# A macaron block with experts on one core: first layernorm's statistics partly on ACT, the last additions shared between engines, a priority for each pair and block

## The chip, the cores and the metric

The kernel runs on one core of a Trainium2 chip. The metric is device time in microseconds, from the launch of the one program to its end; the time given is the median of three runs. The engines are PE (matrix products and transposes), DVE (vector), ACT (activations), POOL (vector work and indirect DMAs) and SP (which only issues DMAs here).

## The reference

All arithmetic is in float32, on x with 2 x 2048 tokens of 256 numbers each:

```python
x = x + 0.5 * ffn(layernorm(x))
x = x + attention(layernorm(x))
x = x + 0.5 * ffn(layernorm(x))

# ffn: 8 experts of width 176, the best 2 for each token
probs = softmax(h @ router_w.T); vals, idx = top_k(probs, 2)
vals = vals / vals.sum(-1)
for each expert e:
    gate, up = split(h @ gate_up_proj[e].T)
    out += weight_of_e * ((silu(gate) * up) @ down_proj[e].T)

# attention: a causal convolution over 3 tokens gives q, k, v of width 64;
# 8 heads of 64, causal softmax within blocks of 128 tokens,
# then two projections (64, 256)
```

## The kernel before, in words

**Stages.** The 4096 tokens are 8 groups of 512, each of 4 tiles of 128 tokens. The first feed-forward (half 1) runs in two chunks, groups 0 to 2 and 3 to 7; then each group's attention; then the second feed-forward (half 2) in chunks of groups 0 to 4 and 5 to 7. In names of tiles, `hs_f1_0_4` is half 1, chunk 0, from slot 4.

**Layernorm.** `layernorm()` makes a group's means and variances half a group (two tiles) at a time: two `bn_stats` (L505) and two `bn_aggr` (L507) on DVE. The power -0.5 is taken on POOL (L520), after an addition on DVE (L515); where ACT does the normalising (L548), POOL also makes a shift (L527, L528), and DVE normalises at L543. The result goes to DRAM (`hd`), and through transposes (L564, copied out as hT) into the router's logits (L638, L652).

**Routing.** `route()` finds the two best experts, counts, and places each token in slots of 128 rows that belong to one expert. This is a long list of small DVE instructions (L697 to L912), then for each pair of token tiles a one-hot step on DVE (L977, L981, L985) and four products (psl, L992), whose sums are the indices (L1010; second chunk L1019, L1023). The table of the slots' experts (L928 to L952) is read by PE and SP into registers, for each pair anew.

**Experts.** `expert()` handles two slots (a pair): POOL gathers their rows by index (L1113, `hs`), PE transposes them (L1124, `ptr`, copied out as hsT), multiplies with gate and up (L1165, `pgu`), ACT does the tanh (L1179), DVE the rest of swiglu (L1185 to L1188), PE transposes (L1195/1196, `pm`, copied out as hmT) and multiplies with the down projection (L1218/1224, `po`), copied out as `ys`. The three copies go through a helper, on ACT at L295 and on DVE at L299. In half 1 the pairs are stored (`yd`) and gathered by `combine()` (POOL L1329, DVE addition L1339). In half 2 POOL scatters them to DRAM (L1240, a put); `gather_all()` then loads, for two tiles of tokens at a time, 512 KB (SP L1283, into one of four buffers "s"), adds four times on DVE (L1304, weight times row plus x) and stores the result (SP L1314).

**Attention.** For each group: convolution (pqk L1515, pv L1537), pvm (L1556), pu (L1609), then four blocks of 128 tokens: scores (ps L1633), mask (L1642, DVE), row maxima (L1651 to L1653, DVE), exponential (L1667, ACT), reciprocal (L1674, DVE), the product with it (L1678, POOL), transposes (pst L1688), context (pcx L1705), projection (pp L1725), and the addition to x (L1735, DVE). POOL adds the projection's bias to x at L1496.

**What sets the order.** Nothing is issued in the order of the source. Each call of `step()` records a piece of work with its cost on one or more engines (the first named is its main engine; another one is taken only where the main one is busy for over 0.3 us longer). `Plan.emit()` then lays all steps out as a list on every engine, in modelled time: of the steps that could start first, the one of highest priority goes. Priority is the longest modelled path to the end plus a bias, which the table `RANK` sets for each stage. Steps also wait for free buffers of their pool. The list of each engine is then fixed, so on the chip an instruction that waits holds up all that stand behind it on its engine. While the plan finds PE idle in the first 60 us, it fills the gap with `warm` products.

The rule for the choice of engine, and the bias of the pairs:

```python
main = next(iter(s.costs))
if e != main and free[main] < t + 0.3:
    continue
...
plan.bias = RANK["expert1"][c] - 0.1 * RANK["slope1"][c] * i
expert(k, i, min(2, k.NSL - i))
```

Of the kernel before, what the change touches and what calls it, by code (L numbers as in the profile page):

```python
# [10 lines left out]
AF = mybir.ActivationFunctionType  # L11
# [10 lines left out]
NS = TB // P  # L22
# [35 lines left out]


RANK = {  # L60
    "logits1": (2852, 2216, 3314, 3481, 1963, 1827, 1743, 3136),
    "route1": (2091, 3734),
    "expert1": (1442, 1598),
    "fold": -360,
    "combine1": (18, 283, -268, 352, -138, -584, -694, -436),
    "attention": (31, 66, 458, -108, 359, -125, -210, -806),
    "logits2": (342, -30, -17, 461, -107, 728, -336, -232),
    "route2": (-70, 1682),
    "expert2": (-795, -757),
    "combine2": (-359, -989),  # L70
    "slope1": (168, 1),
    "slope2": (10, 184),
}


# [171 lines left out]
def kernel(  # L247
# [38 lines left out]
    def work(tag, shape, name, dt=F32):  # L286
        return buf(pools[tag], tag, shape, name, dt)
# [208 lines left out]
    def layernorm(g, nm, store, hT, off, wide=None):  # L496
        stats = work("stats", [P, NS, 6], f"stats_{nm}")
        mv = work("mv", [P, NS, 2], f"mv_{nm}")
        rstd = work("rstd", [P, NS], f"rstd_{nm}")
        for i in range(NH):  # L500
            ts = range(2 * i, 2 * i + 2)

            def stat(e, ts=ts):
                for t in ts:
                    nc.vector.bn_stats(stats.t[:, t, :], X[g].t[:, t, :])  # L505
                for t in ts:
                    nc.vector.bn_aggr(mv.t[:, t, :], stats.t[:, t, :])  # L507

            step(
                {"DVE": 0.89}, stat, reads=[(X[g], t) for t in ts],  # L510
                writes=[(stats, i), (mv, i)],
            )
        step(
            {"DVE": 0.1},
            lambda e: nc.vector.tensor_scalar(rstd.t, mv.t[:, :, 1], EPS, None, ALU.add),  # L515
            reads=[mv], writes=[rstd],
        )
        step(
            {"POOL": 1.1},
            lambda e: nc.gpsimd.tensor_tensor(rstd.t, rstd.t, mhalf.t, ALU.pow),  # L520
            reads=[mhalf], writes=[rstd],
        )

        shift = work("shift", [P, NS], f"shift_{nm}")

        def shifts(e):
            nc.gpsimd.tensor_tensor(shift.t, mv.t[:, :, 0], rstd.t, ALU.mult)  # L527
            nc.gpsimd.tensor_scalar(shift.t, shift.t, -1.0, None, ALU.mult)  # L528

        step({"POOL": 0.25}, shifts, reads=[mv, rstd], writes=[shift])  # L530
        for i in range(NH):
            if wide is None:
                h = work("h", [P, 2, D], f"h_{nm}_{i}")
                h_ = lambda h=h: h.t
            else:
                h, h_ = wide, lambda i=i: wide.t[:, 2 * i : 2 * i + 2, :]
            hp = (h, i)

            def norm(e, i=i, h_=h_):
                for j in range(2):  # L540
                    t = 2 * i + j
                    if e == "DVE":
                        nc.vector.tensor_scalar(  # L543
                            h_()[:, j, :], X[g].t[:, t, :], mv.t[:, t, 0:1],
                            rstd.t[:, t : t + 1], ALU.subtract, ALU.mult,
                        )
                    else:
                        nc.scalar.activation(  # L548
                            h_()[:, j, :], X[g].t[:, t, :], AF.Identity,
                            bias=shift.t[:, t : t + 1], scale=rstd.t[:, t : t + 1],  # L550
                        )

            step(
                {"ACT": 0.98, "DVE": 0.65}, norm,
                reads=[rstd, mv, shift] + [(X[g], 2 * i + j) for j in range(2)], writes=[hp],
            )
            if store is not None:
                store(i, hp, h_)
            pt = bank([P, KD, 2, P], f"pt_{nm}_{i}")

            def turn(e, h_=h_, pt=pt):
                for c in range(KD):
                    for j in range(2):
                        nc.tensor.transpose(  # L564
                            pt.t[:, c, j, :], h_()[:, j, c * P : (c + 1) * P], ident.t
                        )

            step({"PE": 0.52}, turn, reads=[hp, ident], writes=[pt], room=[hT])
            o0 = off + 2 * i * P
            step(  # L570
                {"ACT": 0.49, "DVE": 0.6},
                lambda e, pt=pt, o0=o0: copy(
                    e, hT.t[:, :, o0 : o0 + 2 * P].rearrange("p c (t q) -> p c t q", q=P),
                    pt.t,
                ),
                reads=[pt], writes=[(hT, i)],
            )
        return rstd
# [511 lines left out]
    def expert(k, i0, n):  # L1090
        nm = f"{k.nm}_{i0}"

        beside = k.half == 2 and k.first

        def copied(act, dve):
            return {"ACT": act, "DVE": dve} if beside else {"DVE": dve, "ACT": act}
# [174 lines left out]
    def gather_all(g):  # L1271

        k = chunk_of(g, 2)
        want = [(k, i) for i in range(k.NSL)]
        if k.first:
            want += [(k.next, i) for i in range(NLEFT)]
        for t in range(0, NS, 2):
            n = (g - k.g0) * NS + t
            yg = work("s", [P, 2, 2, D], f"y2_{g}_{t}")

            def get(e, t=t, yg=yg):
                r0 = 2 * (g * TB + t * P)
                ins = nc.sync.dma_start(  # L1283
                    yg.t, Y2.t[r0 : r0 + 4 * P, :].rearrange("(t p j) d -> p t j d", p=P, j=2)
                )
                apart(ins, [m for w, m in Y2.puts.items() if w not in want])
                for w in want:
                    tc.add_manual_dep(
                        ins.ins, Y2.puts[w],
                        mybir.DependencyInfo(  # L1290
                            mybir.DependencyClass.Sync, mybir.DependencyReason.DATA
                        ),
                        reason="its rows",
                    )
                Y2.gets.append(ins.ins.name)

            step(
                {"SP": 0.5}, get, reads=[(Y2, w) for w in want], writes=[yg], lat=LAND, kb=512
            )
            for i in range(2):  # L1300
                for j in range(2):
                    step(
                        {"DVE": 0.43},
                        lambda e, i=i, j=j, n=n, t=t, yg=yg: nc.vector.scalar_tensor_tensor(  # L1304
                            X[g].t[:, t + i, :], yg.t[:, i, j, :],
                            k.wt.t[:, j, n + i : n + i + 1], X[g].t[:, t + i, :],
                            ALU.mult, ALU.add,
                        ),
                        reads=[yg, k.wt], writes=[(X[g], t + i)],
                    )  # L1310
            r0 = g * TB + t * P
            step(
                {"SP": 0.35},
                lambda e, r0=r0, t=t: nc.sync.dma_start(  # L1314
                    out[r0 : r0 + 2 * P, :].rearrange("(t p) d -> p t d", p=P),
                    X[g].t[:, t : t + 2, :],
                ),
                reads=[(X[g], t), (X[g], t + 1)], lat=LAND, kb=256,
            )
# [154 lines left out]
    def attention(g):  # L1474
# [145 lines left out]
                )  # L1620

        oT = work("oT", [P, NS // 2, P], f"oT_{nm}")
        for b in range(NS):
            bs = slice(b * P, (b + 1) * P)

            s = work("s", [P, HEADS, P], f"s_{nm}_{b}")
# [113 lines left out]
    for c in range(2):  # L1740
        k = chunks[1, c]
        for g in range(k.g0, k.g1):
            plan.bias = RANK["logits1"][g]
            logits(g, 1)
            if c == 0 and g == k.g1 - 1:
                loads_then(k.rows)
        plan.bias = RANK["route1"][c]
        route(k)
        for i in range(0, k.NSL, 2):
            plan.bias = RANK["expert1"][c] - 0.1 * RANK["slope1"][c] * i  # L1750
            expert(k, i, min(2, k.NSL - i))
            if c == 0 and i == 0:
                step({"PE": 0.1}, ones_once, reads=[(k.y, 0), ones16], writes=[warm])
                plan.bias = RANK["expert1"][c] + 500.0
                hand_on(k)
                loads_last(k)
# [9 lines left out]
    for c in range(2):  # L1766
        k = chunks[2, c]
        plan.bias = RANK["route2"][c]
        route(k)
        for i in range(0, k.NSL, 2):  # L1770
            plan.bias = RANK["expert2"][c] - 0.1 * RANK["slope2"][c] * i
            expert(k, i, min(2, k.NSL - i))
            if c == 0 and i == 0:
                hand_on(k)
# [66 lines left out]
```

## Time and profile before

| what | before |
| --- | --- |
| median of three runs | 714.97 us (713.4 to 716.16) |
| the profiled execution | 717.35 us, of which its span is 715.6 |
| PE busy | 650.9 us (91%), 4837 instructions |
| DVE busy | 512.4 us (72%), 1408 instructions |
| ACT busy | 317.6 us (44%), 1008 instructions |
| POOL busy | 398.6 us (56%), 458 instructions |
| chain that ended last | PE 54%, DVE 33%, issue 4%, POOL 4%, DMA 4%, ACT 1% |
| mean granted clock of PE | 0.946 |

The span runs from the first to the last instruction of the profiled execution. Busy shares are averages over stages that have different limits, so they don't say what bounds the kernel. The chain is followed back from the last instruction through whatever released each one. In a row of a group of instructions, the numbers before the bar are the total and the mean of one, and behind it stands the idle time of the engine ahead of them with what ended it.

### The profile page before, as it was taken

To read this page: it belongs to the slowest core of one execution; us is meant where nothing else is said; L and a number is where in the kernel's file an instruction comes from. 1 tells how busy PE (TensorE), PEld (TensorE's weight loads), DVE (VectorE), ACT (ScalarE), POOL (GpSimd) and SP (SyncE) were. 2 spreads that over 40 slices of the span, in tenths; PEclk is the share of its full clock that TensorE was granted. 3 is DMA by queue.
4 is the path that set the end of the run, shared out by engine and by line. 5 is a ranking of instruction groups with operands and counts; after the bars stand their busy time and mean duration, and the time that the engine had idled before them with its cause. 6 is when DMAs were issued, how large, how long until landed. Compare 5 with 4: busy or idle time off the path is not lost.

```text
span 715.6 us, 14981 instructions
## 1 busy us (share of the span) xinstructions
PE 650.9 (91%) x4837; PEld 492.9 (69%) x4837; DVE 512.4 (72%) x1408; ACT 317.6 (44%) x1008; POOL 398.6 (56%) x458
## 2 busy tenths in 40 slices
PE   6888989999999999799989997979999799999960
PEld 4647868888888754657566564657888687888840
DVE  5884984455448959998999789999845933447735
ACT  4224322222222437495997857448944233223220
POOL 4037207643337877787744622158867477777650
PEclk9699989999999999899999998979999899999995
DMA  9916616564456343023100110027224234439937
GB/s 295 305 63 188 225 49 181 181 181 142 131 139 177 123 119 88 24 59 105 38 32 30 29 47 15 17 80 231 86 87 140 65 118 131 126 110 322 323 109 264
DMA packets 64891, 92.59 MB, mean 129 GB/s; under 512 B 10128, under 2 KB 50352, under 8 KB 64720
## 3 DMA queue, kind: packets, MB, share of 16 engines
q1 hardware_dynamic: 51520, 55.31, 24.1%
q0 software_dynamic: 13296, 36.32, 17.3%
q8 instruction: 41, 0.67, 0.4%
q14 instruction: 34, 0.28, 0.1%
HBM read 56.47 MB, written 37.22 MB: 131 GB/s over the span
## 4 chain that ended last, share of the span: by engine, by line
PE 54%; DVE 33%; issue 4%; POOL 4%; DMA 4%; ACT 1%; SPq 0%; POOLq 0%; DVEq 0%; ACTq 0%
PE pgu_f L1165 20%; PE po_f L1218 8%; PE po_f L1224 5%; DVE nmx_a L1651 4%; DVE s_a L1642 4%; PE ptr_f L1124 3%; DVE x L1339 2%; PE pm_f L1195 2%; DVE oh_f L977 2%; PE pst_a L1688 2%; PE pcx_a L1705 2%; DVE stats_f L505 2%; PE pt_f L564 2%; POOL yg_f L1329 1%; DVE ot_f L985 1%
## 5 line engine op out<-in xcount | busy, mean ns | idle before, releaser
L1113 POOL DMA_INDIRECT hs_f<-hd_f,idx_f x142 | 137.1, 965 | 129.0 <-PE ptr_f L1124 40.6
L1165 PE MATMUL pgu_f<-wx,hsT_f 128*128 x1136 | 184.0, 318 | 1.8 <-DVE hsT_f L299 0.8
L1165 PEld LDWEIGHTS pgu_f<-wx,hsT_f 128*128 128x128 f32 x1136 | 172.7, 193 | 7.5 <-issue 2.6
L1667 ACT ACTIVATE s_a<-s_a,nmx_a 128x128 f32<-128x128 f32 x256 | 98.9, 392 | 11.8 <-DVE nmx_a L1653 11.2
L1678 POOL TENSOR_TENSOR s_a<-s_a,sm_a 128x512 f32<-128x512 f32 x64 | 67.0, 1069 | 61.4 <-DVE sm_a L1674 59.7
L1240 POOL DMA_INDIRECT y<-ys_f,dst_f x71 | 71.0, 1000 | 33.5 <-ACT ys_f L295 13.9
L295 ACT COPY ys_f<-po_f 128x256 f32<-128x256 f32 x123 | 40.8, 375 | 109.8 <-PE po_f L1224 92.4
L1179 ACT ACTIVATE hm_f<-pgu_f 128x352 f32<-128x352 f32 (+1 forms) x72 | 33.0, 460 | 108.8 <-PE pgu_f L1165 106.5
L1218 PE MATMUL po_f<-wx,hmT_f 128*128 x284 | 76.6, 392 | 0.7 <-DVE hmT_f L299 0.7
L1185 DVE SCALAR_TENSOR_TENSOR hm_f<-hm_f,pgu_f 128x352 f32<-128x352 f32 (+1 forms) x72 | 36.7, 510 | 56.2 <-ACT hm_f L1179 55.9
L1329 POOL DMA_INDIRECT yg_f<-yd_f,posi_f x64 | 61.7, 964 | 24.9 <-issue 15.3
L1218 PEld LDWEIGHTS po_f<-wx,hmT_f 128*128 128x128 f32 x284 | 49.5, 192 | 10.6 <-DVE hm_f L1188 3.3
L299 DVE COPY hmT_f<-pm_f 128x384 f32<-128x384 f32 x40 | 22.2, 556 | 44.1 <-PE pm_f L1196 43.9
L1224 PE MATMUL po_f<-wd_f,hmT_f 48*128 48x256 f32 x284 | 51.1, 432 | 0.0
L1339 DVE SCALAR_TENSOR_TENSOR x<-yg_f,wt_f,x 128x256 f32<-128x256 f32 x64 | 41.6, 674 | 11.0 <-DMA yg_f<-yd_f,posi_f 11.0
L1667 ACT ACTIVATION_READ_ACCUMULATOR s_a<-s_a,nmx_a 128x1 f32 x256 | 49.0, 192 | 0.0
L1515 PE MATMUL pqk_a<-haT_a,cw 128*128 128x512 f32 x96 | 46.3, 630 | 0.5 <-ACT haT_a L295 0.5
L1124 PE MATMUL ptr_f<-ident,hs_f 128*128 128x128 f32 x284 | 42.2, 276 | 2.4 <-DMA hs_f<-hd_f,idx_f 2.4
L1688 PE MATMUL pst_a<-ident,s_a 128*128 128x128 f32 x256 | 37.1, 287 | 4.5 <-DVE vm_a L299 2.9
L1642 DVE TENSOR_TENSOR s_a<-ps_a,later 128x512 f32<-128x512 f32 x64 | 40.5, 678 | 0.0
L1688 PEld LDWEIGHTS pst_a<-ident,s_a 128*128 128x128 f32 x256 | 29.2, 146 | 16.3 <-issue 9.5
L1651 DVE TENSOR_REDUCE nmx_a<-s_a 128x8 f32<-128x1024 f32 x32 | 38.7, 1210 | 0.2
(235 smaller groups left out, 1228.0 us busy)
## 6 DMA issues: line engine op xcount, KB each, us to landing
yd_f<-ys_f SPq DMA_DIRECT2D x42, 256.0 KB, 3.6
hd_f<-h_f SPq DMA_DIRECT2D x32, 256.0 KB, 3.2
y<-y SPq DMA_DIRECT2D x16, 512.0 KB, 5.3
wd_f<-in_w_down SPq DMA_DIRECT2D x142, 48.0 KB, 2.7
x<-in_x SPq DMA_DIRECT2D x16, 256.0 KB, 7.0
out<-x SPq DMA_DIRECT2D x16, 256.0 KB, 3.2
hd_f<-hd_f SPq DMA_DIRECT2D x1, 2560.0 KB
hs_f<-hd_f,idx_f POOLq DMA_INDIRECT x142
```

The source lines that it names most:

```text
L1113: lambda e, i=i, hs_=hs_: nc.gpsimd.indirect_dma_start(out=hs_(), out_offset=None, in_=k.h.t[:, :], in_offset=bass.IndirectOffsetOnAxis(ap ...
L1124: nc.tensor.transpose(pt.t[:, d, j, :], hs_()[:, d * P : (d + 1) * P], ident.t)
L1165: nc.tensor.matmul(pgu[f].t[:, j, :], hsT.t[:, d, j, :], wx.t[:, bass.ds(at + d * GU + f * H, H)], start=(d == 0), stop=(d == KD - 1),)
L1218: nc.tensor.matmul(po[j].t, hmT.t[:, j, :], wx.t[:, bass.ds(at + KD * GU, D)], start=True, stop=False,)
L1224: nc.tensor.matmul(po[j].t, hmT.t[r, n, :], wd.t[r, :], start=False, stop=True)
L1240: ins = nc.gpsimd.indirect_dma_start(out=Y2.t[:, :], out_offset=bass.IndirectOffsetOnAxis(ap=k.dst.t[:, i : i + 1], axis=0), in_=ys.t[:, j ...
L1329: lambda e, j=j, n=n, yg=yg: nc.gpsimd.indirect_dma_start(out=yg.t, out_offset=None, in_=k.y.t[:, :], in_offset=bass.IndirectOffsetOnAxis( ...
L1642: lambda e, h=hd[i], s=s, p=ps[i]: nc.vector.tensor_tensor(s.t[:, h, :], p.t, later.t.to_broadcast([P, NPAIR, P]), ALU.add,),
L1651: nc.vector.tensor_reduce(nmx.t, s.t, AX.X, ALU.max)
L1667: nc.scalar.activation(s.t[:, n, :], s.t[:, n, :], AF.Exp, bias=nmx.t[:, n : n + 1], accum_out=sm.t[:, c : c + 1],)
L1678: lambda e, s=s, sm=sm, h=hd[i]: nc.gpsimd.tensor_tensor(s.t[:, h, :], s.t[:, h, :], sm.t.unsqueeze(2).to_broadcast([P, NPAIR, P]), ALU.mu ...
L1688: nc.tensor.transpose(pt.t[:, c, :], s.t[:, i * NPAIR + c, :], ident.t)
```

## The change

The table `RANK` gets other numbers for all stages, and five new lists: one bias for each pair of slots (`pairs10` to `pairs21`, for half and chunk) and one for each of the 32 attention blocks (`blocks`). For groups 3 to 7 the statistics step of the first layernorm may go to ACT where DVE is busy; there it is made of sums that two activations accumulate, with the tile that takes the normalised rows later as scratch. The plan puts five half groups there: both of group 4, both of group 5, and one of group 6. In half 1's first chunk the copies hsT, hmT and ys get ACT as main engine (so far only half 2's first chunk had that). In the last chunk's additions 4 of 12 tiles of tokens are scaled in place on ACT (two activations) and added on POOL (two additions) instead of two times on DVE.

```diff
 RANK = {
-    "logits1": (2852, 2216, 3314, 3481, 1963, 1827, 1743, 3136),
+    "logits1": (3004, 3634, 3185, 2969, 1036, 1648, 1568, 3176),
...
+    "pairs10": (-38, 306, 165, -360, -358, -360, -818, 76, -597),
...
+    "blocks": (4, 4, 5, 4, 4, 4, 4, 4, 4, 4, 4, 4, 7, 4, -141, 4, 8, 494, -157, -7, 0, 0, 0, 0, 0, 0, 0, 0, 0, 114, -26, -1),
...
+        shared = wide is not None and g >= first
...
             def stat(e, ts=ts):
+                if e == "ACT":
...
+                    a = nc.scalar.activation
+                    st, m = stats.t, slice(ts[0], ts[-1] + 1)
+                    for t in ts:
+                        a(wide.t[:, t, :], X[g].t[:, t, :], AF.Identity, accum_out=st[:, t, 0:1])
+                    a(mv.t[:, m, 0], st[:, m, 0], AF.Copy, scale=1.0 / D)
+                    a(st[:, m, 1], st[:, m, 0], AF.Copy, scale=-1.0 / D)
+                    for t in ts:
+                        a(
+                            wide.t[:, t, :], X[g].t[:, t, :], AF.Square, bias=st[:, t, 1:2],
+                            accum_out=st[:, t, 2:3],
+                        )
+                    a(mv.t[:, m, 1], st[:, m, 2], AF.Copy, scale=1.0 / D)
+                    return
...
             step(
-                {"DVE": 0.89}, stat, reads=[(X[g], t) for t in ts],
-                writes=[(stats, i), (mv, i)],
+                {"DVE": 0.89, "ACT": 2.6} if shared else {"DVE": 0.89}, stat,
...
-        beside = k.half == 2 and k.first
+        beside = k.first
...
+                if not k.first and (NS * (g - k.g0) + t + i) % 3 == 2:
...
+                            nc.scalar.activation(
+                                yg.t[:, i, j, :], yg.t[:, i, j, :], AF.Copy,
+                                scale=k.wt.t[:, j, n + i : n + i + 1],
+                            )
...
+                            nc.gpsimd.tensor_tensor(
+                                X[g].t[:, t + i, :], X[g].t[:, t + i, :], yg.t[:, i, j, :],
+                                ALU.add,
+                            )
...
+            plan.bias = bias0 + RANK["blocks"][NS * g + b]
...
+                + RANK["pairs1" + str(c)][i // 2]
...
+                + RANK["pairs2" + str(c)][i // 2]
```

In the changed kernel's lists the pairs of half 1's first chunk come in the order 2, 4, 0, 14, 6, 8, 10, 16, 12 (before 0, 2, 4 and so on to 16), those of its second chunk begin 40, 2, 0, 46, 42, those of half 2 begin 0, 8, 6, 2, 4 and 2, 0, 4, 6, 10.

## The prediction

> **What bounds the kernel now.** I first read the page's strip of 40 slices (17.9 us each): it shows that no one engine bounds the whole span.
>
> ```profile
> PE   6888989999999999799989997979999799999960
> DVE  5884984455448959998999789999845933447735
> PEclk9699989999999999899999998979999899999995
> ```
>
> PE is at 9 almost everywhere, so a step on another engine can save time only where PE's digit falls or where its clock falls: slices 1 to 6, 16, 24, 26, 31 and the end. There DVE is often the full one. A PE at a lower clock counts as busy, so the last line (the clock in tenths) belongs to the first. The second view is busy time by stage.
>
> ```profile
> 0.00:57.00 57.00, 46.24 (x381) 29.27 (x385) 41.30 (x182) 19.60 (x40) 18.37 (x51) 0.88 0.69 217
> 57.00:86.00 29.00, 26.51 (x203) 22.60 (x195) 19.90 (x65) 11.46 (x29) 14.68 (x17) 0.94 0.63 199
> 86.00:228.00 142.00, 138.31 (x891) 116.29 (x892) 81.42 (x190) 33.51 (x90) 62.44 (x66) 0.98 0.51 149
> 228.00:455.00 227.00, 212.84 (x1719) 137.82 (x1719) 205.28 (x526) 150.16 (x539) 140.01 (x155) 0.96 0.21 61
> 455.00:550.00 95.00, 90.08 (x794) 72.86 (x789) 72.18 (x200) 59.00 (x206) 63.20 (x69) 0.95 0.36 113
> 550.00:682.00 132.00, 126.71 (x809) 106.98 (x808) 77.32 (x212) 40.67 (x100) 90.22 (x91) 0.97 0.53 169
> 682.00:715.60 33.60, 10.23 (x58) 7.06 (x57) 15.01 (x36) 3.23 (x9) 9.70 (x10) 0.71 0.55 190
> ```
>
> Columns after the window and its length: busy time of PE, weight loads, DVE, ACT, POOL, then PE's clock and DMA. The experts' stages (86 to 228, 550 to 682) are PE's own: 138.31 of 142 at clock 0.98. The attention (228 to 455) is DVE's: 205.28 of 227. The prologue (to 57) hangs on DVE, ACT idles for 37 us of it. The last 33.6 us are puts, gathers and last additions. Third view, what PE waits for up to 120 us:
>
> ```profile
> PE psl_f L992 <- DVE ot_f L985: 4.2, 5, 1.1
> PE ptr_f L1124 <- DMA hs_f<-hd_f,idx_f: 2.4, 1, 2.4
> PE pm_f L1195 <- DVE hm_f L1188: 0.9, 1, 0.9
> ```
>
> All three stand behind DVE's list: one-hots, the first chunk's indices (which release the gathers), swiglu.
>
> **The statistics on ACT.** DVE's groups between 28 and 107 us:
>
> ```profile
> L977 DVE TENSOR_TENSOR oh_f<-col,prf_f 128x512 f16<-128x512 f16 x16 | 11.0, 685 | 2.5 <-PE psl_f L992 2.4
> L505 DVE BATCH_NORM_STATS2 stats_f<-x 128x6 f32<-128x256 f32 x20 | 7.3, 408 | 0.0
> L507 DVE BATCH_NORM_AGGREGATE mv_f<-stats_f 128x2 f32<-128x6 f32 x20 | 3.0, 173 | 0.0
> ```
>
> (7.3 + 3.0) / 10 half groups is 1.03 us each; in the changed order five half groups (all of groups 4 and 5, half of 6) leave DVE: 5.2 us. ACT's seven instructions for a half group have no row here. From below: four 128x256 activations at 0.545 (two take 1.09 in the norm's row) and three small ones at 0.2 are 2.8 us. From above: with the 0.192 of the accumulator read that follows each exponential, 4 x 0.74 + 0.6 = 3.6. I take 3.4, since these have accumulators as the exponential has; 14 to 18 us in all, beside 37 idle.
>
> What it brings is the first gather. Before, the indices come at 49.30 on DVE, the gathers start on POOL at 49.77 and 54.52, the second lands at 59.98, and the first pgu starts at 62.57. In the new order the indices no longer follow group 4's statistics (1.73), a norm (0.63) and the expert table's first part (1.06), but a copy of 0.69: 46.6. But POOL now issues the power of groups 7, 5 and 4 (1.65 each with its shift) ahead of the first gather, and group 4's waits for ACT, which can't start before the loads (about 34 us) and then needs 4 x 3.4 = 13.6 us for groups 5 and 4: 47.6 at best, 50 with what ACT does between. With 1.65 for the power the first gather starts at 49.3 to 52, the second 1.27 later, as nothing is between them now. So 50.5 to 53.3 instead of 54.52, and pgu comes 1.2 to 4 us earlier. A norm and a copy that now queue on ACT ahead of hsT (1.09 + 0.59) may take half of it: I take **-2.0** (-4 to 0).
>
> Then chunk 0 gives some of it back. The order of pairs becomes 2, 4, 0, 14, 6, 8, 10, 16, 12, and DVE's swiglu of the fourth pair stands behind six one-hot steps instead of four. Before, DVE goes from the third swiglu's end (75.4) to the fourth's start (91.4) in 16.0 us; two more one-hot steps at 1.32 and three small ones (0.6) make it 19.2. PE idles 3.5 of 15 us at 85 to 100 now, at clock 0.77. It would idle up to 3.2 more; but one swiglu fewer (1.22) is then ahead of chunk 1's indices, and a pair (4.8 us of PE) is kept for the gathers' latency. I take **+1.5** (0 to +5). The sum to 115 us is -0.5.
>
> **Copies of chunk 0 to ACT** (hsT, hmT, ys): 5 hsT at 0.69 leave DVE, but elsewhere it gets 7 ys at 0.42, 2 hT and others; by the counts DVE's work from 57 us on is about 1.5 us more, mostly in expert stages that PE bounds. **0**; if that cover were gone, 1.5.
>
> **Pairs out of order.** From 115 to 228 us and from 550 on PE does the same pairs, two per 9.65 us. The table of experts is read seven times more on PE's queue (38 to 45 loads, 0.33 us median): nothing where the sequencer is ahead, 7 x 0.33 = 2.3 where not. Between 86 and 228 us PE has only 3.7 us without work, so most loads are hidden: I take **+0.5** (0 to 2.3). The gathers of these pairs move with them on POOL, which is busy for 62 of 142 us.
>
> **Attention blocks.** The orders are nearly the same: blocks 2 of group 0, 1 of 4 and 1 of 7 go first, 3 of 3 before 2. DVE bounds here and has but 16 us without work between 285 and 515 us, 7.6 of them between 395 and 415, where PE runs a full 20 us: DVE waits there for pu (2.6) and pt (1.9) and less for others. In the new order the first pu of group 5 stands ahead of the context matmuls instead of behind them, so I take that wait: **-2.6**. The bounds: -7.6 if all of that idle goes, +4 if a swap opens one more idle stretch like 465 to 475 (4.2 us of PE).
>
> **The last additions.** Before:
>
> ```profile
> 698.04 5.67 SPq L1283 DMA_DIRECT2D y<-y  x5
> 704.93 0.36 SPq L1283 DMA_DIRECT2D y<-y  x1
> 701.65 8.01 DVE L1304 SCALAR_TENSOR_TENSOR x<-y,wt_f,x 128x256 f32<-128x256 f32 x20 [8.32 <-DMA y<-y]
> 710.25 1.67 DVE L1304 SCALAR_TENSOR_TENSOR x<-y,wt_f,x 128x256 f32<-128x256 f32 x4 [0.59 <-DMA y<-y]
> ```
>
> Four gathers of 512 KB fill the four buffers, the last two wait for a buffer to come free, and the sixth (704.93) sets the end: 5.3 to land, 1.67 of additions, then a store of 3.2. DVE's 8 saved additions (3.4 us) lie in the wait for DMA and save nothing. What counts is when the first and second buffers are free. Now: 4 additions each, 1.65 and 3.28 after the first landing. Changed: ACT scales (1.09), POOL adds two of 128x256 (half of the 1.07 to 1.30 of its 128x512 rows, 1.2 with starts): 2.4 and 3.6. That is +0.3 on the sixth, if POOL and DVE don't hinder each other. The trace has a case where they do:
>
> ```profile
> 245.30 3.15 DVE L1339 SCALAR_TENSOR_TENSOR x<-yg_f,wt_f,x 128x256 f32<-128x256 f32 x1
> 245.67 2.49 POOL L1496 TENSOR_TENSOR x<-x,pb 128x512 f32<-128x512 f32 x2
> ```
>
> The same addition takes 0.478 in the median: beside POOL's two it ends only when they end. So up to five DVE additions (2.1 us) may come between POOL's: +2.4 on the sixth. Besides, four pairs' last products now all come after the last pgu, so eight puts stand in a row at 1.27 instead of six; ACT's and DVE's copies come earlier for two of them: +0.6 (0 to 2.5). I take **+1.5** for the tail (0 to +4.5).
>
> The Trainium skill, "SBUF — State Buffer", section "Who interferes with whom", has a rule for this row: a DVE instruction with two inputs in SBUF and a GpSimd instruction that reads SBUF exclude each other for the whole instruction. It speaks against this part; by it the tail would be +0.6 + 2.4 = 3.0 instead of +0.9 without it, and the row agrees. "TensorE: Matmul & The Clock Gate", Part 1, says that the clock has only a half and a full step and changes after a window of about 3.4 us; by that a stall that crosses one more window would cost about 1.7 us (an estimate from that page) beyond itself.
>
> **The sum.** -0.5 + 0 + 0.5 - 2.6 + 1.5 = -1.1 on the profiled execution (717.35, its span 715.6): 716.25. That execution is 2.4 above the median of the runs (714.97), so I put it at **713.9** against that median. A measurement of this kernel can tell about 0.5% (3.6 us) from no change, so this counts as the same.
>
> **Rivals.**
> 1. *The new priorities clear the stalls.* For it: PE and DVE both idle in the attention, so a better order has 7.6 us to win there without less work, and pgu could come the full 4 us earlier with no stall behind. -4 + 0 + 0.5 - 7.6 + 1.5 = -9.6: **705.4** (702 to 710). Against it: the orders differ in few places, and DVE is at 19.7 of 20 from 300 to 390.
> 2. *Slower: PE stalls for chunk 0's swiglu.* Place: 85 to 110 us. If the fourth, fifth and sixth pair wait behind the one-hots and PE comes back at half clock each time, +5 for it, nothing from the first gather, and the rest as above: 5 + 0.5 - 2.6 + 1.5 = +4.4, and up to +7 if pu's wait stays: **719.4** (717.5 to 723). It decides from about 4 us more PE idle than the 3.5 there now.
> 3. *The statistics' move brings nothing*, because group 4's power, now ahead of the first gather, waits for ACT: first pgu at 62.5 again. 0 + 1.5 + 0.5 - 2.6 + 1.5 = +0.9: **715.9** (713 to 718).
>
> **Chances.** The forecast 0.36 (711 to 717), rival 1 0.32, rival 2 0.23, rival 3 0.09. Faster by over 0.5% (under 711.4): rival 1 and 0.04 of the forecast, 0.36. Slower by over 0.5% (over 718.5): 0.19 of rival 2 and 0.03 of others, 0.22. Same: 0.42. The range, 704 to 720.5, leaves out a third of rival 1 and of rival 2, some 0.18. The forecast's own range is 711 to 717.
>
> **What would show it.** First gather on POOL near 51 and first pgu near 60.5 (step 1); PE idle between 85 and 105 of 5 us or more against 3.5 (rival 2); first pgu of chunk 1 near 114 against 114.78; DVE idle in the stretch of groups 3 and 5 of about 5 instead of 7.6 (none: rival 1); the sixth of the last gathers issued 7.5 to 9.5 us after the last put has landed (now 697.78 to 704.93, 7.15), with DVE additions of over 1 us beside POOL's (tail). I am wrong if PE's idle time in the attention moves by more than 4 us either way, or if ACT's statistics take over 4.5 us a half group.

## The result and the profile after

The changed kernel takes **721.24 us** in the median of 7 runs (717.8 to 722.35), the kernel before 715.91 in 7 runs beside it: ratio 1.0066 (95% interval 1.0043 to 1.0088), so it is slower by about 0.7%. A second series (e1 below) gave the same ratio: 1.0066 (1.0047 to 1.0085).

The profiled execution of the changed kernel happens to be the shortest of its seven (717.8, span 716.1), and that of the kernel before is longer than most of its own (717.35). Laid side by side they differ by 0.5 us and hide the loss. So I compare stages over several profiles, and show first the views that answer to those of before. The strips of the page:

```profile
PE   7898979999999999799999998889999799999960
DVE  5883973443457959998999889999756843447735
PEclk9799979999999999799999999989999899999995
```

What is new stands above all in slice 6 (about 90 to 107 us): PE 7 where it had 8, at clock 7 where it had 8. The same stages as before (columns as there):

```profile
0.00:57.00 57.00, 47.23 (x407) 29.06 (x407) 40.07 (x168) 29.74 (x92) 20.00 (x54) 0.88 0.74 234
57.00:86.00 29.00, 27.04 (x174) 23.39 (x175) 19.18 (x65) 11.79 (x28) 12.68 (x15) 0.88 0.40 117
86.00:228.00 142.00, 137.18 (x881) 116.17 (x882) 75.08 (x179) 37.30 (x95) 61.65 (x65) 0.96 0.53 158
...
682.00:715.60 33.60, 9.82 (x54) 6.65 (x53) 15.22 (x29) 5.58 (x13) 14.48 (x16) 0.71 0.54 184
```

The first stage has the move that was meant: ACT 29.74 us instead of 19.60, DVE 40.07 instead of 41.30. DVE lost 5.2 us of statistics and gained other work that came earlier. What PE waits for up to 120 us, and DVE's statistics between 28 and 107:

```profile
PE psl_f L1015 <- DVE ot_f L1008: 4.3, 5, 1.7
...
PE ptr_f L1147 <- DMA hs_f<-hd_f,idx_f: 1.9, 2, 1.3
...
PE pm_f L1218 <- DVE hm_f L1211: 1.3, 2, 0.9
```

```profile
L527 DVE BATCH_NORM_STATS2 stats_f<-x 128x6 f32<-128x256 f32 x10 | 3.7, 409 | 0.0
```

Half of the `bn_stats` are gone (10 of 20), and the three waits are still there: the one-hots still end last. The way to the first pgu in this profile, first on POOL:

```profile
44.60 1.04 POOL L543 TENSOR_TENSOR rstd_f<-rstd_f,mhalf 128x4 f32<-128x4 f32 x1 [11.75 <-DVE end_f L960]
...
51.91 0.95 POOL L1136 DMA_INDIRECT hs_f<-hd_f,idx_f  x1 [0.30 <-issue]
...
55.38 1.05 POOL L543 TENSOR_TENSOR rstd_f<-rstd_f,mhalf 128x4 f32<-128x4 f32 x1
```

Then on PE and on ACT:

```profile
55.40 0.44 PE L1147 MATMUL ptr_f<-ident,hs_f 128*128 128x128 f32 x2 [1.28 <-DMA hs_f<-hd_f,idx_f]
```

```profile
57.07 1.09 ACT L571 ACTIVATE h_f<-x,shift_f,rstd_f 128x256 f32<-128x256 f32 x2 [2.75 <-POOL shift_f L551]
58.06 0.56 ACT L300 COPY hsT_f<-ptr_f 128x512 f32<-128x512 f32 x1
```

The second gather (51.91) has landed at 55.40, but ACT copies its rows only at 58.06: ahead of this copy its list has the normalising of group 6, which waits 2.75 us for a power that stands on POOL behind four gathers. In the kernel before the first pgu starts 2.0 to 2.5 us after the second gather has landed (three profiles), here 5.2 (60.61). The last additions:

```profile
698.16 6.44 SPq L1306 DMA_DIRECT2D y<-y  x5
...
705.97 0.36 SPq L1306 DMA_DIRECT2D y<-y  x1
```

```profile
701.76 1.01 DVE L1347 SCALAR_TENSOR_TENSOR x<-y,wt_f,x 128x256 f32<-128x256 f32 x2 [9.17 <-DMA y<-y]
703.11 4.84 DVE L1347 SCALAR_TENSOR_TENSOR x<-y,wt_f,x 128x256 f32<-128x256 f32 x6 [0.34 <-DMA y<-y]
708.27 2.19 DVE L1347 SCALAR_TENSOR_TENSOR x<-y,wt_f,x 128x256 f32<-128x256 f32 x4 [0.32 <-DMA y<-y]
711.06 1.67 DVE L1347 SCALAR_TENSOR_TENSOR x<-y,wt_f,x 128x256 f32<-128x256 f32 x4 [0.59 <-DMA y<-y]
```

The sixth gather goes out 7.81 us after the first instead of 6.89. Where POOL adds too, six of DVE's additions take 4.84 us (0.81 each); the four at the end, alone, take 0.42 each as before.

**Where the time went, by stage.** Means over the profiles of each kernel and of those experiments that can't touch the stage (3 to 7 each; us):

| stage | before | changed | difference |
| --- | --- | --- | --- |
| start to group 3's transposes (PE) | 38.15 | 37.64 | -0.5 |
| from there to the first pgu | 23.1 | 24.5 | +1.3 |
| to chunk 1's first pgu | 51.5 | 54.9 | +3.4 |
| to the first convolution product | 132.4 | 132.9 | +0.5 |
| to the last projection product | 283.0 | 282.8 | -0.2 |
| to the last expert product (po) | 163.3 | 162.1 | -1.2 |
| to the end | 22.7 | 24.2 | +1.5 |
| sum | | | +4.8 |

The sum agrees with the difference of the medians (4.6 to 5.3). In single profiles the first row alone runs from 36.2 to 38.8, and the changed kernel's last expert product comes 160.7 to 164.3 after the last projection, so the gain in that row is not clear of the spread.

The third row can be divided where DVE has made the indices of chunk 1, which release the next gathers. Before:

```profile
106.11 0.19 DVE L1023 TENSOR_SCALAR idx_f<-psl_f 128x40 int32<-128x40 f32 x1
```

```profile
110.36 1.46 PE L1165 MATMUL pgu_f<-wx,hsT_f 128*128 x8
114.78 1.43 PE L1165 MATMUL pgu_f<-wx,hsT_f 128*128 x8 [0.22 <-ACT hmT_f L295]
```

Changed:

```profile
103.82 0.19 DVE L1046 TENSOR_SCALAR idx_f<-psl_f 128x40 int32<-128x40 f32 x1
```

```profile
105.59 1.36 PE L1188 MATMUL pgu_f<-wx,hsT_f 128*128 x8
109.14 2.65 PE L1188 MATMUL pgu_f<-wx,hsT_f 128*128 x16
115.85 4.44 PE L1188 MATMUL pgu_f<-wx,hsT_f 128*128 x28
```

From the first pgu to the end of the indices both kernels take 43.1 us in the mean of three profiles (42.0 to 43.7 before, 42.4 to 43.4 changed). From there to chunk 1's first pgu (114.78 and 115.85) it is 8.5 us before and 11.8 changed. So all of the 3.4 us stand behind the indices, where the changed kernel's PE has no gap, but 24 products with gate and up of chunk 0 left instead of 8: one pair more. These two lengths hardly vary: 8.5 to 8.6 in all five profiles with the lists of the kernel before, 11.8 in all nine with the changed lists, those with moved steps included.

### The profile page after: what moved, and what is told of

The parts are those of the page before. It is cut to its first block, busy times and chain, and to the rows that moved or that the text cites. A ratio compares the mean times of both kernels' runs of the same rounds, so it can differ in the third digit from the quotient of the medians.

```text
span 716.1 us, 15066 instructions
## 1 busy us (share of the span) xinstructions
PE 651.4 (91%) x4838; PEld 492.2 (69%) x4838; DVE 510.1 (71%) x1388; ACT 331.9 (46%) x1063; POOL 405.7 (57%) x466
## 4 chain that ended last, share of the span: by engine, by line
PE 55%; DVE 28%; DMA 5%; ACT 4%; POOL 4%; issue 3%; DVEq 0%; POOLq 0%; SPq 0%; ACTq 0%
PE pgu_f L1188 21%; PE po_f L1241 7%; PE po_f L1247 5%; PE ptr_f L1147 4%; DVE s_a L1687 3%; DVE nmx_a L1696 3%; PE pcx_a L1750 3%; PE pm_f L1218 2%; PE pst_a L1733 2%; DVE oh_f L1000 2%; PE ps_a L1678 2%; DVE x L1382 2%; DMA y<-y 2%; PE pt_f L587 1%; DMA yg_f<-yd_f,posi_f 1%
## 5 line engine op out<-in xcount | busy, mean ns | idle before, releaser
L1188 PE MATMUL pgu_f<-wx,hsT_f 128*128 x1136 | 186.8, 320 | 2.2 <-ACT hsT_f L300 1.5
L1188 PEld LDWEIGHTS pgu_f<-wx,hsT_f 128*128 128x128 f32 x1136 | 174.8, 195 | 8.2 <-issue 4.2
L1723 POOL TENSOR_TENSOR s_a<-s_a,sm_a 128x512 f32<-128x512 f32 x64 | 67.1, 1067 | 54.9 <-DVE sm_a L1719 38.4
L1263 POOL DMA_INDIRECT y<-ys_f,dst_f x71 | 71.4, 1006 | 30.5 <-issue 13.6
L300 ACT COPY ys_f<-po_f 128x256 f32<-128x256 f32 x116 | 38.8, 375 | 107.0 <-PE po_f L1247 100.1
L1208 DVE SCALAR_TENSOR_TENSOR hm_f<-hm_f,pgu_f 128x352 f32<-128x352 f32 (+1 forms) x72 | 36.7, 510 | 54.3 <-ACT hm_f L1202 54.2
L1733 PE MATMUL pst_a<-ident,s_a 128*128 128x128 f32 x256 | 38.6, 289 | 6.3 <-DVE vm_a L304 2.9
L543 POOL TENSOR_TENSOR rstd_f<-rstd_f,mhalf 128x4 f32<-128x4 f32 x16 | 17.1, 1070 | 42.4 <-DVE jmp_f L899 18.8
```

What stands on the lines that cost most here:

```text
L1188: nc.tensor.matmul(pgu[f].t[:, j, :], hsT.t[:, d, j, :], wx.t[:, bass.ds(at + d * GU + f * H, H)], start=(d == 0), stop=(d == KD - 1),)
L1263: ins = nc.gpsimd.indirect_dma_start(out=Y2.t[:, :], out_offset=bass.IndirectOffsetOnAxis(ap=k.dst.t[:, i : i + 1], axis=0), in_=ys.t[:, j ...
L1723: lambda e, s=s, sm=sm, h=hd[i]: nc.gpsimd.tensor_tensor(s.t[:, h, :], s.t[:, h, :], sm.t.unsqueeze(2).to_broadcast([P, NPAIR, P]), ALU.mu ...
L1733: nc.tensor.transpose(pt.t[:, c, :], s.t[:, i * NPAIR + c, :], ident.t)
```

## The experiments

Where an edit keeps the lists, the plan is made as in its kernel and only the named instructions are moved or given to another engine. Otherwise the plan lays everything out anew. The edits are shortened to their sense.

**e1, the changed kernel again.**

> The changed kernel once more, unaltered. Its profiled execution (717.8 us) was the shortest of its seven (median 721.24), so it does not show where the 5 us over the kernel before come from. Theory T (tail): POOL's and DVE's last additions exclude each other, and the sixth of the last gathers, 1.0 us later in the profile we have, is 3 to 6 us later in an ordinary execution; then this run's time is near 721 and its stages up to the last product (po last near 692) are as before. Theory M (middle): the executions differ in the expert or attention stages, and the last product itself ends at 695 to 698.

It gave 720.84, the profile 718.45 of span. Both theories fall: all stages from the first pgu on are within 1 us of the first profile, and the 2.3 us between the two profiles arise before 40 us. PE's filler (the `warm` products) ahead of group 3's transposes, in the first profile and in this one:

```profile
30.95 5.39 PE L409 MATMUL warm<-ones 128*128 128x512 f16 x18
```

```profile
31.63 7.02 PE L409 MATMUL warm<-ones 128*128 128x512 f16 x18
```

The same 18 products take 5.39 or 7.02 us and start 0.7 us apart; in these two profiles what stands behind them shifts as a whole, and the ends lie 2.4 us apart.

**e2, the last additions on DVE again** (lists kept):

```diff
-  nc.scalar.activation(yg, yg, AF.Copy, scale=weight)     # ACT, 2x
-  nc.gpsimd.tensor_tensor(x, x, yg, ALU.add)              # POOL, 2x
+  nc.vector.scalar_tensor_tensor(x, yg, weight, x, ...)   # DVE, 2x, at POOL's place
```

> The changed kernel with the order of all lists kept, but the shared last additions are made on DVE again, at the place where POOL had them. Theory T: the time falls to that of the kernel before, 715 to 717 (ratio 0.998 to 1.003). Theory M: it stays near 720 to 721 (at most 1 us less).

719.54, ratio 1.0050 (1.0034 to 1.0067): 1.3 us less than e1, with intervals that overlap, so at most a small part of the loss. From the last expert product to the end it takes 23.9 instead of 24.0 to 24.1. The sixth gather goes out 0.4 us earlier, but the last one lands no sooner. On e1's POOL the eight additions took

```profile
704.71 7.05 POOL L1337 TENSOR_TENSOR x<-x,y 128x256 f32<-128x256 f32 x8 [5.96 <-ACT y L1328]
```

0.88 each. Sixteen additions on DVE and eight on POOL end as late as 24 on DVE.

**e3, the statistics on DVE again** (lists kept; the five half groups at the places ACT had them):

> The changed kernel with the order of all lists kept, but the five half groups' statistics are made on DVE at the place where ACT had them. Theory of the prediction (statistics on ACT win about 2 us at the first pgu): first pgu at 62 to 64 instead of 60.6, total 1 to 3 us longer than the changed kernel. Rival (they bring nothing, DVE's list ends last anyway): the same within 1 us.

722.63, ratio 1.0098 (1.0067 to 1.0129). First gather 17.05 us after group 3's transposes instead of 14.20, first pgu 2.9 us later: in the changed lists ACT is the better place for this work.

**e4, the kernel before again.**

> The kernel before, unaltered, as a second profile of it and as a measure of the noise: ratio 1.000 within 0.3%. If its milestones (first pgu 62.6, first pgu of chunk 1 114.8, first pqk 247.1, last po 692.9) move by more than 1 us from one execution to the next, then single profiles can't tell steps of that size apart.

716.32, ratio 1.0002 (0.9987 to 1.0016). Its first pgu stands at 60.50, not 62.57, with the first gather at the same time (49.62 and 49.77). So the profile that my prediction was worked out on had its first pgu 2 us late, by a slower second gather (5.46 us to land, here 4.10) and a lower clock.

**f1, the statistics alone may go to ACT; f2, the priorities alone** (the kernel before, laid out anew):

```diff
 # f1, in layernorm()
+  {"DVE": 0.89, "ACT": 2.6} if shared else {"DVE": 0.89}
 # f2: RANK as in the change, with pairs and blocks, and nothing else of it
```

> The kernel before with one part of the change alone: the first layernorm's statistics may go to ACT; priorities, copies and last additions as before (the plan lays the lists out anew: five half groups again go to ACT; the first gather on POOL has only group 3's power ahead of it, the second gather stands behind three powers). Theory A (what costs is the order of the prologue, where ACT's statistics and three powers stand ahead of the first gather): the first gather comes at 47 to 49 us, the first pgu at 60 to 62, the total 714 to 717, no worse than before. Theory B (the statistics on ACT cost as such, since they stand on ACT behind a copy that waits for PE's filler): first gather at 51 or later, total 718 to 720.

> The kernel before with the new priorities alone (table, pairs, blocks); statistics, copies and last additions as before. Theory A (the order costs, mainly the first gather behind three powers and the pairs of chunk 0): first pgu at 63 or later, 2 to 3 us more than before between the first pgu and chunk 1's first pgu, the stretch from the last product to the end 1.2 us longer, attention and half 2 about 2 us shorter, total 719 to 723. Theory B (the statistics on ACT cost): total 714 to 717.

f1: 736.2, ratio 1.0272 (1.0246 to 1.0298). f2: 726.81, ratio 1.0141 (1.0113 to 1.0169). Neither theory holds. f1 does have its first gather at 45.7 and first pgu at 59.0, earlier than both kernels, and loses some 20 us later: 4.5 up to chunk 1's first pgu, 3.5 in chunk 1, 3.3 ahead of the first scores, 9 in the attention. f2 is as before up to 530 us and loses 8.8 in half 2's experts. A plan laid out anew with priorities tuned for another one says nothing of the part that was changed, so from here on the lists are kept.

**f3 and f4, half the filler** (lists kept):

```diff
-  for _ in range(int(0.7 * us / (0.43 if warmer.cold else 0.22))):
+  for _ in range(int(0.7 * us / 0.43)):
```

> The changed kernel with about half as many filler products on PE after the first gap (the filler of 18 products at 31 us takes 5.3 to 7.0 us at the low clock, while the plan meant 5.6 at most); order of all lists kept. Theory W (the end of the filler sets group 3's transposes, the copy hT that heads ACT's statistics, and so the first gather): first gather and first pgu 2 to 3 us earlier, total 717 to 718.5, and the spread between executions, which follows the filler's 5.3 or 7.0, falls. Rival (PE's lower clock after a thinner filler costs as much as is won): total 720 to 722.

> The kernel before with the same thinner filler, order kept. Theory W: DVE's list hangs less on the transposes than ACT's statistics do, yet first gather 1 to 3 us earlier, total 713 to 715. Rival (lower clock): 716 to 718.

f3: 719.62, ratio 1.0040 (1.0022 to 1.0057), 1.2 less than e1. f4: 716.09, ratio 0.9993 (0.9974 to 1.0012), no difference that can be told. Group 3's transposes come at 34.5 in both. In f3 the first gather comes at 50.18 all the same: POOL's first power waits for DVE, whose list has no gap from 33 us on, until 44.41 (44.60 in the first profile). f3's time lies between the ranges of both theories. In f4's profile the first pgu is 2.8 us ahead of e4's, and most of it is lost in the attention (285.7 instead of 283.0), at two waits of 1.6 to 2.2 us for a combine gather and for transposes.

**g1, the first pair's gathers ahead of two powers** (lists kept but POOL's):

```diff
+  plan.ahead: gathers 2, 3 of chunk 0 ahead of group 5's power
```

> The changed kernel, all lists kept but POOL's: the first pair's two gathers go ahead of groups 5's and 4's power, right behind group 7's. Theory A (the gather stands behind three powers): the first gather comes 3 to 4.5 us earlier after group 3's transposes (14.2 us after them now, 10 to 11 then), and the total falls by 1 to 2.5 us, to 718.5 to 720. Rival (POOL's whole list up to group 6's power sets the first pgu, in whatever order): first gather earlier, first pgu the same within 0.7 us, total 720 to 721.5.

723.48, ratio 1.0100 (1.0077 to 1.0123): the rival's mechanism, and worse. The first gather comes 10.8 us after the transposes instead of 14.2, but the first pgu 25.2 instead of 24.5. POOL's list in g1:

```profile
49.63 1.23 POOL L1142 DMA_INDIRECT hs_f<-hd_f,idx_f  x1 [0.79 <-DVE h_f L572]
51.17 0.95 POOL L1142 DMA_INDIRECT hs_f<-hd_f,idx_f  x1 [0.30 <-issue]
52.13 1.06 POOL L549 TENSOR_TENSOR rstd_f<-rstd_f,mhalf 128x4 f32<-128x4 f32 x1
...
53.78 1.07 POOL L549 TENSOR_TENSOR rstd_f<-rstd_f,mhalf 128x4 f32<-128x4 f32 x1
...
55.61 1.09 POOL L1142 DMA_INDIRECT hs_f<-hd_f,idx_f  x1 [0.17 <-issue]
57.01 0.95 POOL L1142 DMA_INDIRECT hs_f<-hd_f,idx_f  x1 [0.30 <-issue]
57.98 1.05 POOL L549 TENSOR_TENSOR rstd_f<-rstd_f,mhalf 128x4 f32<-128x4 f32 x1
```

POOL has hardly a gap from 49.63 on (0.3 us at most). What comes earlier there puts something else later: PE then waits 3.2 us for DVE's normalised rows, which need the powers, and the first pgu stands behind their transposes. Group 6's power (57.98) comes 19.2 us after the transposes of group 3, as it does without the move (55.38 in the first profile), and the first pgu stays behind it. No run moved this power alone.

**g2, swiglu ahead of the one-hots** (lists kept but DVE's):

```diff
+  plan.ahead: swiglu 14 ahead of one-hot 4, swiglu 6 of 6, swiglu 8 of 8
```

> The changed kernel, all lists kept but DVE's: in chunk 0 the swiglu of the fourth, fifth and sixth pair go two one-hot steps earlier each, where the kernel before has them. Theory C (these swiglus behind the one-hots are what lengthens the stretch from the first pgu to chunk 1's first pgu from 52 to 54.3 to 55.3 us): that stretch falls to 52 to 53.2, total 718 to 719.5. Rival (DVE's list up to the second chunk's indices is as long either way, and these end last): stretch 54 to 55.5, total 720 to 721.5.

724.34, ratio 1.0108 (1.0082 to 1.0134). The stretch is 55.9 us, not 52 to 53.2: theory C falls. Putting swiglu first only makes PE wait for the one-hots instead (psl 7.6 us, in e1 5.7).

**g3, the statistics on ACT with the lists of the kernel before:**

```diff
 def stat(e):
+  if group in (4, 5) or (group == 6 and second half): the ACT version, at DVE's place
```

> The kernel before, all lists kept, but the same five half groups' statistics run on ACT at the places where DVE had them (DVE's list loses them, nothing is laid out anew). Theory S (statistics on ACT do help if nothing else moves): first gather 1.5 to 1.7 us earlier after group 3's transposes (11.4 now), first pgu 1 to 2 us earlier, total 714 to 715.5. Rival (ACT's statistics hold up group 7's normalising and copies on ACT's list, and with them the first pgu): first gather earlier, first pgu 0 to 2 us later, total 716.5 to 719.

719.41, ratio 1.0046 (1.0026 to 1.0066): the rival. First gather 1.0 us earlier (10.42 after the transposes), first pgu 3.4 to 5.3 later (27.6 instead of 24.2 and 22.3). What PE waits for between 36 and 66 us there:

```profile
PE pl_f L654 <- ACT hT_f L295: 4.2, 1, 4.2
```

Group 7's copies hT stand on ACT behind group 5's statistics (5 us for a group); before, they came at once, and PE's logits behind them. The second gather comes 1.7 us later too (17.8 after the transposes instead of 16.2), since the power ahead of it on POOL waits 2.67 us for those statistics.

**g4, the last additions shared in the kernel before** (lists kept, one run):

> The kernel before, all lists kept, but 4 of the last 12 tiles' additions are scaled on ACT and added on POOL. From the first of the last six gathers' issue to the end it takes 17.2 to 17.6 us now. Theory P (DVE's and POOL's additions shut each other out): the sixth gather is issued 7.5 to 8.0 us after the first instead of 6.9 to 7.0, and the end comes at 17.6 to 18.2; DVE's additions beside POOL's take 0.7 to 0.9 us. Rival (they run side by side): DVE's additions 0.48, sixth gather after 6.5 to 7.2, end at 17.0 to 17.5.

719.64 in one run. From the first of the six gathers to the end: 21.5 us, more than theory P had, though the sixth gather goes out after 7.30. DVE's additions beside POOL's take 0.83 to 0.94 us, as theory P had them, and here the last gather's tiles have a shared one:

```profile
709.34 1.00 DVE L1310 SCALAR_TENSOR_TENSOR x<-y,wt_f,x 128x256 f32<-128x256 f32 x2 [0.72 <-DMA y<-y]
```

```profile
710.00 1.72 POOL L1308 TENSOR_TENSOR x<-x,y 128x256 f32<-128x256 f32 x2 [1.67 <-ACT y L1307]
```

A chain ACT, POOL, store then stands at the very end. The changed kernel avoids that: its last two gathers are added on DVE alone. But only 1.4 to 1.8 us of the loss stand ahead of the last store's issue (15.3 after the first gather, before 13.5 and 13.9); from there to the end it is 6.2 us instead of 3.7, and what lengthened that in this one run is open.

**i1, the last logits ahead of the second pair** (lists kept but PE's):

```diff
+  plan.later: gate and up products of pair 4 behind group 6's logits transpose
```

> The changed kernel, all lists kept but PE's: the gate and up products of the second pair go behind the last logits' transpose (group 6) instead of ahead of it. In the profiles of the changed kernel DVE's routing of chunk 1 starts 6.2 to 6.6 us after the first pgu (4.3 to 5.4 in the kernel before), since this transpose stands behind two pairs' products; its indices end at 42.4 to 43.6 although one swiglu fewer is ahead of them, and then three pairs are left instead of two. Theory R (the late start of the routing lengthens chunk 0): routing starts at 4.3 to 4.8, indices at 40.5 to 42, the stretch from the first pgu to chunk 1's first pgu falls from 54.3 to 55.3 to 52.5 to 53.7, total 718 to 720. Rival (PE's remaining three pairs set that end, not the indices): indices earlier, stretch 54 to 55.5, total 720 to 721.5.

719.91, ratio 1.0059 (1.0037 to 1.0081), 0.9 less than e1, which the spread of both does not separate. The stretch itself is clear: 53.0 instead of 54.3 and 55.3, with the routing starting 5.2 after the first pgu instead of 6.2 to 6.4 and the indices at 41.2 instead of 42.4 to 43.4. PE in e1 and in i1:

```profile
62.96 2.63 PE L1188 MATMUL pgu_f<-wx,hsT_f 128*128 x16 [1.88 <-ACT hT_f L300]
65.52 0.64 PE L661 MATMUL pl_f<-hT_f,wr 128*32 128x128 f32 x16
66.09 0.33 PE L675 MATMUL plt_f<-ident,ls_f 128*128 128x128 f32 x1
66.26 2.55 PE L1188 MATMUL pgu_f<-wx,hsT_f 128*128 x16
68.65 0.27 PE L675 MATMUL plt_f<-ident,ls_f 128*128 128x128 f32 x1
```

```profile
64.81 0.33 PE L681 MATMUL plt_f<-ident,ls_f 128*128 128x128 f32 x1
65.49 0.33 PE L681 MATMUL plt_f<-ident,ls_f 128*128 128x128 f32 x1 [0.36 <-ACT ls_f L306]
65.66 2.58 PE L1194 MATMUL pgu_f<-wx,hsT_f 128*128 x16
```

In e1 the last logits (the second plt row) wait for a second pair's 2.55 us, and DVE's whole routing of chunk 1 with them. What i1 wins lies ahead of the indices; from their end to chunk 1's first pgu it is 11.8 us here too. So it wins time where nothing had been lost: in the kernel before the routing starts after 4.3 to 5.4 us, and the indices come no earlier than in the changed kernel.

**i2, three repairs at once** (i1, e2 and f3 together):

> The changed kernel with three repairs at once, lists kept: the last logits' transpose ahead of the second pair (as in i1), the last additions all on DVE (as in e2), the thinner filler (as in f3). If what the single runs gave adds up (e2 -1.3, f3 -1.2 against 720.84, i1 by theory R -1.5), the total is 716 to 717.5, the kernel before's; if it stays at 719 or more, the rest of the loss lies elsewhere (first gather behind three powers, PE's three pairs).

716.67, ratio 1.0007 (0.9989 to 1.0025): the kernel before's time. The single gains (1.3, 1.2, 0.9) add up to 3.4, and 4.2 was found. But its profile does not show the routing's part: there the first pair's products take 4.22 us instead of 2.78 in i1, at a granted clock of 0.60 instead of 0.94, the routing starts at 6.6 and the stretch is 55.3, so the share of each repair is not settled. Nothing that I ran beats both kernels.

## Why the prediction was wrong

The forecast was 713.9, "the same"; the change costs 4.6 to 5.3 us. The time lies just above the range (720.5), and above rival 2's 719.4, whose sum was near but whose mechanism was not.

- **Statistics on ACT, first pgu: taken as -2.0, measured +1.3.** This is the step that failed. Counted from group 3's transposes (38.36 in the profile it was worked out on), the first gather was to come after 10.9 to 13.6 us and the second after 12.1 to 14.9. They came after 14.2 and 15.7 in every profile that left this part alone, against 11.4 and 16.2 before; that 50.4 lies in the forecast range is luck, since the transposes were 2.2 us early in that profile (in e1 it is 52.7). The path was another one too: POOL's three powers do not wait for ACT, whose fourth half group is done at 45.9 (the third power starts at 47.91), but for DVE (44.60), and then follow each other without a gap. So the second gather came 0.4 us earlier, not 1.2 to 4, and the rest of the step, "a norm and a copy that now queue on ACT ahead of hsT (1.09 + 0.59)", was priced by its own length: that norm waits 2.75 to 2.78 us in five profiles for group 6's power, which POOL takes behind four gathers, and PE's transposes of the same group stand ahead of pgu. g1 fits: it moves the gathers but not this power, and the pgu comes no earlier. The statistics alone are not what costs: in the changed lists they are better on ACT (e3), in those of before worse (g3). Besides, the 62.57 that I counted from was 2 us late in that execution (e4). Rival 3 (statistics bring nothing) came nearest, but not for its reason, a power that waits for ACT.
- **Chunk 0: +1.5, measured +3.4.** The sign and the place were right: PE idles 6.0 to 7.4 us from the first pgu to chunk 1's first, instead of 3.8 to 4.3. The cause was not: g2 refutes the swiglus behind six one-hots, which was also rival 2's. The prediction counted the "pair (4.8 us of PE)" that "is kept for the gathers' latency" as a help. This pair is where the time is: the indices come no later after the first pgu than before, and behind them PE works 11.8 us without a gap instead of 8.5. It idles ahead of the indices, for the one-hots, while this pair is still to do. No run moved that pair alone. What a stall at a lower clock costs beyond itself (1.7 us in my estimate) no run separates either.
- **Copies and pairs: 0 and +0.5, measured +0.5** up to the convolution. Half 2 is 1.2 us shorter, which I had at 0, within a spread of 3.6 in single profiles; which of the edits does it is open, since f2 (priorities alone) loses there.
- **Attention: -2.6, measured -0.2.** DVE's wait for pu did fall, from 2.6 to 1.1, and that for pt (1.9) is gone. Others took their place between 285 and 515 us:

```profile
DVE x L1780 <- PE pp_a L1770: 2.8, 2, 1.4
DVE x L1382 <- DMA yg_f<-yd_f,posi_f: 2.2, 1, 2.2
DVE haT_a L1531 <- PE pl_f L661: 1.5, 1, 1.5
DVE s_a L1687 <- PE ps_a L1678: 1.3, 4, 0.7
DVE u_a L306 <- PE pu_a L1652: 1.1, 2, 0.8
```

  DVE's busy time in that window is 214.57 us instead of 214.06: a wait that goes is worth nothing while the same work waits for the same PE in another place. Rival 1 falls with it. The argument that I held against it was right in the main only: between 320 and 340 us DVE was busy for 18.19 of 20 us, not 19.7. And the low slices that I listed from the strip as 16, 24, 26 and 31 are the 17th, 25th, 27th and 32nd.
- **Tail: +1.5, measured +1.5.** The sum fits by parts that do not. The eight puts in a row are there (last put 3.4 us after the last product instead of 2.5, +0.9 for the 0.6 taken). The rest of the sum was to be a later sixth gather, and it is 0.9 later, but e2 puts only 0.4 of that on the shared additions, and the end moves by 0.1 to 0.2. That POOL and DVE exclude each other, as the Trainium skill's page "SBUF — State Buffer" says in "Who interferes with whom", this case shows: 0.81 instead of 0.42 for DVE's additions beside POOL's.

## What to carry to other kernels

Before pricing a step that comes earlier, follow every list that it shares up to the end of the stage: here a gather came a little earlier, and a step ahead of its copy on ACT waited for a power behind that gather on POOL. Ask of each reordered stage how much work of the bounding engine is left behind its last wait: here one pair more, 3.4 us. Take the base of the sum from two profiles at least: the first 60 us of this kernel move by 2 us from one execution to the next. Where a planner sets the order, keep its lists and move single steps to learn what a part of a change does; a new plan with priorities tuned for another one was 10 to 20 us worse.

## What the runs showed of the hardware

- The 18 filler products of 128x512 on PE take 5.4 to 7.0 us from one execution to the next (5.39 and 7.02 in the changed kernel, 5.49 and 6.90 in the one before). In the changed kernel's two profiles a shift of 2.3 us behind them was 2.4 at the end; in those of the kernel before the transposes behind them came within 0.2 us of each other.
- ACT's statistics for half a group take 2.6 us (four activations with accumulators at 0.40 to 0.51, each with 0.19 to read the accumulator, mostly beside the next one), where I had taken 3.4.
- A DVE addition of 128x256 beside a POOL addition of the same size took 0.81 us instead of 0.42, and POOL's 0.88, so the two engines together did no more than DVE alone.
